# A ceiling on the planner's work per step: attention followed by a learned density, on one core

## The chip, the cores and the metric

The kernel runs on one core of a Trainium2 chip. The metric is device time in microseconds (us), the median of several executions. Beside the timed runs there is one profiled execution; all views below are of that one.

## What is computed

The input `x` has 8 images of 192 channels and 64 x 64 points, in float32. Two layers follow each other, each a group norm, a function and a residual:

```python
b, c, h, w = x.shape
q = prelu(conv1x1(x, w1, b1), a1)      # 24 channels
k = prelu(conv1x1(x, w2, b2), a2)      # 24 channels
v = prelu(conv1x1(x, wa, ba), aa)      # 192 channels
score = softmax(einsum('bnc,bcm->bnm', q, k), axis=2)   # 4096 x 4096
out = einsum('bnm,bmc->bnc', score, v)
...
# layer 1, for each channel, at xr - 0.5 and at xr + 0.5
for i in range(4):                      # widths 1, 3, 3, 3, 1
    logits = einsum('cij,cjn->cin', softplus(ms[i]), logits) + bs[i]
    if i < 3:
        logits = logits + tanh(fs[i]) * tanh(logits)
likelihood = maximum(abs(sigmoid(sign * upper) - sigmoid(sign * lower)), 1e-6)
...
x = x + attention(group_norm(x))
x = x + density(group_norm(x))
```

The attention is matmul work (TensorE), with an exponential for each score (ScalarE) and a row maximum (VectorE). The density is pointwise: chains of activations (ScalarE) and of multiply-adds (VectorE).

## The kernel before, in words

An image's attention is 8 blocks of 512 queries, and each block takes 16 steps of 256 keys: 128 steps an image, 1024 in all. One step `t` of the main loop emits, in this order: the score matmuls of step t + 1 into the one score buffer (`scores`, L780); the matmuls and the reduce of the maxima for a step 22 ahead (`max_step`, L708 and L716; one buffer too); the exponential of step t + 1 on ScalarE (L784), whose result `e` the values are multiplied with; the value matmuls of step t (`attend`, L795); and then everything else, in `work_off`.

Each engine works through its own queue in the order in which instructions were emitted. So what `work_off` puts on ScalarE in step t stands ahead of the exponential of the step after, and what it puts on VectorE stands ahead of the next reduce.

`work_off` sets out three kinds of work. *Due work* was entered with `at(t, fn, cost, act, pe)` for a given step, with planned prices for VectorE, ScalarE and TensorE: norms (L442 to L506), the evacuation of a finished block (L819), the residual (L837), the end of a density tile (tanhs and sign at L1202 and L1204, sizes L1249, stores L1254). `run_due` emits all that is due. A *job* needs a free PSUM bank and starts where one is found (`start_job`); the keys (L620), values (L669), output transposes (L828), turned maxima (L745) and folded weights (L547) of the next or current image are jobs, and their parts become due work of this step and the next ones. *Density work* fills up: `density_step` adds a rate to each engine's credit, and `Unit.step` emits operations while the credit is positive. Due work is taken from the same credit, and TensorE time beyond a plain step is added to it.

A `Unit` is one of 12 parts of an image's density (2 column halves, 3 channel groups, 2 sides), 128 x 1024 elements. It holds a list for ScalarE (17 activations: L1015 and L1024 from the input, L1030 tanh, L1040 scaled, L1072) and one for VectorE (22 multiply-adds, all at L1047). Up to three units are open at a time. An operation is emitted when what it reads was emitted in an earlier step, and when one of 17 buffers is free for it. The density of image b runs beside the attention of image b + 1. That of the last image has no attention beside it: its first mixes are matmuls (L988), and it makes the tail.

VectorE's rate is what is left of the image's density divided by the steps left, at most `MOST` = 3.3 a step; ScalarE's is 2.9. A credit can grow to the rate plus 1.3. The prices are 1.22 for a multiply-add, 1.23 for an activation, 1.05 for a tanh of a later layer. A step's own exponential and reduce are outside these sums.

Of the kernel before, what the change touches and what calls it, by code (L numbers as in the profile page):

```python
# [17 lines left out]
def kernel(  # L18
# [58 lines left out]
    last = B * IMG  # L77
# [40 lines left out]
    for i in range(3):  # L118
        t = xin.tile([128, 3, P], F32, tag=f"xi{i}", name=f"xi{i}")
# [211 lines left out]
        due.setdefault(max(t, now[0]), []).append((fn, cost, act, pe))  # L331

    credit = {"DVE": 0.0, "ACT": 0.0, "PE": 0.0}
    units = deque()
    jobs = []
    stream = [False]
# [40 lines left out]
    def start_job(t):  # L377
        p = t % STEPS
        for n, (rank, make, hold, banks, cols) in enumerate(jobs):
            if stream[0] and (p < 3 or p + max(hold, 1) >= STEPS):  # L380
                continue
            rooms = [(pm, g) for pm, g in homes if sum(k <= t for k in g) >= banks]
            if not rooms:
                if rank < 2:
                    return
                continue
            k = [i for i in (1, 0) if ready[i] <= t and scratch[i][0].shape[1] >= cols]
            if cols and not k:
                continue
            del jobs[n]  # L390
            pm, guest = min(rooms, key=lambda r: max(r[1]))
            at_ = [i for i in range(2) if guest[i] <= t]
            for i in at_[:banks]:
                guest[i] = t + hold + 1
            if cols:
                ready[k[0]] = t + 2
            spot[0] = next(n for n, k in enumerate(turns + others) if k is pm), at_[0]
            parts = make(pm if banks == 2 else pm[:, at_[0], :], scratch[k[0]] if cols else None)
            for i, fn, cost, act, pe in parts:
                at(t + i, fn, cost, act, pe)  # L400
            return
# [5 lines left out]
    def run_due(t):  # L407
        todo = due.get(t, [])
        i = 0
        while i < len(todo):  # L410
            fn, cost, act, pe = todo[i]
            fn()
            credit["DVE"] += pe - cost
            credit["ACT"] += pe - act
            i += 1
        due.pop(t, None)

    def work_off(t, rate):
        now[0] = t
        run_due(t)  # L420
        start_job(t)
        run_due(t)
        held = set()
        for kind, fn in list(loads):
            if free[kind] > 0 and kind not in held:
                loads.remove((kind, fn))
                fn()
            else:
                held.add(kind)
        density_step(t, rate)  # L430
        pool_step()
# [173 lines left out]
    for i in range(2):  # L605
        t = dram.tile([NC, 64, F], F32, tag=f"qd{i}", name=f"qd{i}")
# [259 lines left out]
    COST = {"DVE": 1.22, "ACT": 1.23, "TANH": 1.05, "PE": 6.95}  # L866
# [41 lines left out]
    class Unit:  # L908
# [192 lines left out]
        def step(self, eng, t, older):  # L1101
            todo = self.todo[eng]
            while todo and credit[eng] > 0:
                name, after, fn, makes, frees = todo[0]
                if any(self.at.get(a, t) >= t for a in after if eng != "DVE" or a[0] in "ltu"):
                    return
                if eng == "PE" and not banks:
                    return
                if makes and len(bufs) <= sum(u.need() for u in older) + len(endings):
                    return  # L1110
                todo.popleft()
                if makes:
                    self.take(name, makes)
                fn(name)
                self.at[name] = t
                for k in frees:
                    self.give(k)
                credit[eng] -= COST["TANH" if name[0] == "t" and name[1] else eng]

    def density_step(t, rate):  # L1120
        if units and t < last:

            left = sum(len(u.todo["DVE"]) for u in units if u.key[0] == units[0].key[0])
            rate = left * COST["DVE"] / max(1, (units[0].key[0] + 2) * IMG + 15 - t) + OTHER
            rate = min(rate, MOST)
        act = ACT_RATE if t < last else rate

        for eng, most in (("DVE", rate), ("ACT", act)):
            more = (rate if eng == "DVE" else 0.0) if t >= last else 1.3
            credit[eng] = min(credit[eng] + most, most + more)  # L1130
        credit["PE"] = min(credit["PE"] + rate, rate)
        for eng in ("ACT", "PE", "DVE"):
            order = list(range(min(3 if t < last else 4, len(units))))
            if len(units) == 2 and t < last:

                order.sort(key=lambda n: -len(units[n].todo["DVE"]))
            for n in order:
                units[n].step(eng, t, list(units)[:n])
        for u in [u for u in units if not u.busy()]:
            units.remove(u)  # L1140
# [17 lines left out]
    def pool_step():  # L1158


        if pieces:
            if len(recent) == 2:
                inst = nc.gpsimd.memset(pause, 0.0)  # L1163
                tc.add_manual_dep(
                    inst.ins, recent[0].ins.name,
                    mybir.DependencyInfo(
                        mybir.DependencyClass.Sync, mybir.DependencyReason.DATA
                    ),
                    reason="beside the reduce",
                )  # L1170
            pieces.popleft()()
# [184 lines left out]
    def go_on():  # L1356
        work_off(now[0], 0.0)
        now[0] += 1
# [40 lines left out]
    for t in range(last):  # L1399
        b = t // IMG  # L1400
        if t % IMG == 0:
            within(b, t)
            if b + 1 < B:
                prepare(b + 1, t)
            else:

                diagonals(0, t + 93)
                diagonals(1, t + 104)
                diagonals(2, last - 11)
        now[0] = t  # L1410
        if t % STEPS == 0:
            homes[:] = [(turns[(t // STEPS + 1) % 2], [0, 0])]
        if 3 < t < IMG:
            next(rest, None)
        assert t != IMG or next(rest, 0) == 0
        run = scores(t + 1) if t + 1 < last else None
        max_step(t + LEAD)
        if run:
            run()
        attend(t)  # L1420
        work_off(t, RATE - 1.215)
    t = last
    homes[:] = [(turns[1], [0, 0])]
    while due or units or jobs or loads:

        work_off(t, RATE if (B - 1, 1) in norms else 1.3)
        t += 1
# [38 lines left out]
```

## Time and profile before

| what | us |
|---|---|
| median of 3 runs (4797.65 to 4801.9) | 4800.04 |
| profiled execution, its time | 4801.53 |
| profiled execution, its span | 4799.7 |
| TensorE matmuls busy | 4653.4 |
| VectorE busy | 4179.0 |
| ScalarE busy | 3196.8 |
| end of the last exponential | 4440.9 |

The chain of waits, followed back from the last instruction, spends 86% of the span on TensorE, 7% on VectorE and 5% on ScalarE. The forty slices of the page show 9 tenths for VectorE from the seventh slice on, where the density of the first image begins, and 6 or 7 tenths for ScalarE. TensorE's granted clock is full nearly throughout.

| mean duration of one, ns | |
|---|---|
| exponential, L784 | 1021 |
| activation of the density, L1015, L1024, L1040 | 1236 to 1237 |
| later tanh, L1030 | 1054 |
| multiply-add, L1047 | 1292 to 1314 |
| reduce of the maxima, L716 | 1220 |

In the groups of instructions and in the timelines, a line gives the engine, the line of the kernel, the operation, and out<-in by the kernel's names; in brackets stands the idle time before it and what ended it. ACT is ScalarE, DVE VectorE, PE TensorE, POOL GpSimd. Neighbours on one engine overlap by a tenth of a microsecond or so, so the distance of two starts tells more of a queue than a duration does. Busy TensorE is a modelled figure: a matmul can be shown as running while it waits.

### The profile page before, as it was taken

What the parts mean: (1) busy time and instruction counts of PE and PEld (TensorE: products, weight loads), DVE (VectorE), ACT (ScalarE), POOL (GpSimd) and SP (SyncE); (2) the same over time, 40 slices, a digit from 0 to 9 for tenths busy, and PEclk for the clock granted to TensorE, in tenths of its full rate; (3) what the DMA queues carried; (4) which work ended last, traced back from release to release, by engine and by line L of the source; (5) the groups of instructions that cost most, each with busy time, mean ns of one, the idle gap of its engine ahead of it and who ended that gap; (6) DMA issues with size and microseconds to landing.
All of it is one profiled execution on the core that took longest, in us unless ns stands there. A gap on an engine that the chain in (4) does not pass through costs nothing.

```text
span 4799.7 us, 69014 instructions
## 1 busy us (share of the span) xinstructions
PE 4653.4 (97%) x28432; PEld 3440.0 (72%) x28432; DVE 4179.0 (87%) x4289; ACT 3196.8 (67%) x3665; POOL 856.3 (18%) x842
## 2 busy tenths in 40 slices
PE   7999999999999999999999999999999999999686
PEld 5777777777777777777777777777777777777332
DVE  5433359999999999999999999999999999998788
ACT  2333246777677767776777767777777777777675
POOL 0000001222122211221211221122222132222000
PEclk9999999999999999999999999999999999999898
DMA  2101020111110111010110111101111101000000
GB/s 58 41 18 29 18 48 14 35 28 29 42 27 25 37 39 34 27 44 9 36 46 26 33 40 33 32 19 33 36 38 33 34 13 27 10 12 16 9 13 13
DMA packets 109328, 138.60 MB, mean 29 GB/s; under 512 B 17106, under 2 KB 82132, under 8 KB 109012
## 3 DMA queue, kind: packets, MB, share of 16 engines
q1 hardware_dynamic: 107776, 133.81, 11.4%
q8 instruction: 223, 3.65, 0.3%
q14 instruction: 93, 0.76, 0.1%
q10 hardware_dynamic: 1236, 0.37, 0.0%
HBM read 100.58 MB, written 29.36 MB: 27 GB/s over the span
## 4 chain that ended last, share of the span: by engine, by line
PE 86%; DVE 7%; ACT 5%; issue 1%; DMA 0%; POOL 0%; ACTq 0%; SPq 0%; DVEq 0%; POOLq 0%
PE b L795 53%; PE sc L780 20%; PE b L669 4%; DVE d L1047 4%; PE b L988 2%; PE b L620 2%; DVE rm L716 1%; ACT d L1015 1%; ACT e L784 1%; PE mx_tail L988 1%; PE sc_tail L988 1%; PE b L828 1%; PE mx L708 1%; ACT d L1040 1%; PE b L745 0%
## 5 line engine op out<-in xcount | busy, mean ns | idle before, releaser
L795 PEld LDWEIGHTS b<-v,e 128*128 128x128 f32 x16384 | 2651.8, 190 | 776.9 <-issue 771.6
L795 PE MATMUL b<-v,e 128*128 128x193 f32 x16384 | 2955.7, 334 | 0.0
L784 ACT ACTIVATE e<-sc 128x1024 f32<-128x1024 f32 x1024 | 1045.9, 1021 | 1353.4 <-PE mx L708 1330.8
L716 DVE TENSOR_REDUCE rm<-mx 128x1 f32<-128x1024 f32 x1002 | 1222.3, 1220 | 481.4 <-PE mx L708 472.7
L780 PE MATMUL sc<-q,k 25*128 25x512 f32 x4096 | 1155.1, 640 | 24.2 <-ACT e L784 22.9
L708 PE MATMUL mx<-k,q 24*128 24x512 f32 x4008 | 1130.4, 640 | 0.6 <-DVE rm L716 0.6
L1047 DVE SCALAR_TENSOR_TENSOR d<-d,lc,d 128x1024 f32<-128x1024 f32 x756 | 986.1, 1314 | 12.2
L1047 DVE SCALAR_TENSOR_TENSOR d<-d,wsp,d 128x1024 f32<-128x1024 f32 x684 | 883.3, 1292 | 53.1 <-ACT d L1040 44.7
L1047 DVE SCALAR_TENSOR_TENSOR d<-d,tf,d 128x1024 f32<-128x1024 f32 x540 | 687.5, 1292 | 0.4 <-ACT d L1030 0.4
L1163 POOL MEMSET pause<- 128x1 f32 x408 | 40.0, 98 | 3613.2 <-DVE d L1047 3613.2
L1030 ACT ACTIVATE d<-d 128x1024 f32<-128x1024 f32 x540 | 568.2, 1054 | 42.6 <-DVE d L1047 40.8
L780 PEld LDWEIGHTS sc<-q,k 25*128 25x128 f32 x4096 | 306.2, 183 | 252.4 <-issue 175.8
L1040 ACT ACTIVATE d<-d,cb,wsp 128x1024 f32<-128x1024 f32 x348 | 429.9, 1236 | 4.3 <-DVE d L1047 3.3
L1015 ACT ACTIVATE d<-xc,bn,wn 128x1024 f32<-128x1024 f32 x288 | 354.0, 1236 | 7.7 <-issue 5.9
L1078 POOL TENSOR_TENSOR d<-d,d 128x512 f32<-128x512 f32 x168 | 331.8, 1975 | 47.7 <-ACT d L1072 46.6
L1024 ACT ACTIVATE d<-xc,bn,wn 128x1024 f32<-128x1024 f32 x252 | 311.8, 1237 | 0.0
L708 PEld LDWEIGHTS mx<-k,q 24*128 24x128 f32 x4008 | 299.8, 183 | 7.3 <-DVE rm L716 6.7
L1198 POOL TENSOR_TENSOR d<-d,d 128x512 f32<-128x512 f32 x80 | 173.0, 2163 | 0.0
L1210 POOL TENSOR_TENSOR d<-d,d 128x512 f32<-128x512 f32 x80 | 163.2, 2040 | 0.5 <-issue 0.5
L1218 POOL TENSOR_TENSOR d<-d,d 128x512 f32<-128x512 f32 x80 | 157.6, 1970 | 2.5 <-POOL pause L1163 0.9
L669 PE MATMUL b<-wv,xi 64*128 64x192 f32 x1344 | 139.5, 340 | 0.0
L669 PEld LDWEIGHTS b<-wv,xi 64*128 64x128 f32 x1344 | 106.5, 186 | 25.4 <-issue 21.5
(155 smaller groups left out, 2303.9 us busy)
## 6 DMA issues: line engine op xcount, KB each, us to landing
xi<-in_x_dram SPq DMA_DIRECT2D x280, 192.0 KB, 3.5
xc<-in_x_dram SPq DMA_DIRECT2D x64, 384.0 KB, 7.1
out_dram<-xc SPq DMA_DIRECT2D x94, 256.0 KB, 3.1
q<-qd SPq DMA_DIRECT2D x128, 128.0 KB, 2.7
k<-kq SPq DMA_DIRECT2D x64, 64.0 KB, 1.9
qd<-kq SPq DMA_DIRECT2D x64, 64.0 KB, 2.0
d<-in_x_dram SPq DMA_DIRECT2D x16, 192.0 KB, 4.1
out_dram<-xc SPq DMA_DIRECT2D x4, 128.0 KB
```

What stands on the lines that cost most here:

```text
L669: nc.tensor.matmul(pv[:, s, 0:C], lhsT=t[p, g, k * 128 : k * 128 + 128] if g < 3 else one_row[p], rhs=wf["v", b][p, g, :] if g < 3 else wf ...
L708: nc.tensor.matmul(sc[:, s, :], lhsT=tile_of(qt[b, n // 2], n, j)[r], rhs=kt[b][r, u : u + F], start=True, stop=True,)
L716: nc.vector.tensor_reduce(out=rowmax[b, n][:, j, k : k + 1], in_=sc, axis=AX.XY, op=ALU.max)
L780: nc.tensor.matmul(sc[:, s, :], lhsT=kt[b][r, k : k + 128], rhs=qt[b, n // 2][r, :, u : u + 256], start=True, stop=True,)
L784: return lambda: nc.scalar.activation(e, sc, AF.Exp)
L795: nc.tensor.matmul(a[:, j, 0 : C + 1], lhsT=e[:, s, j * 128 : j * 128 + 128], rhs=v[:, s, p % 4, :], start=p == 0 and s == 0 and j % 2 == ...
L1015: nc.scalar.activation(self.buf[k], self.src(), AF.Tanh, bias=bn[:, s, g, 0, i : i + 1], scale=wn[:, g, 0, i : i + 1],)
L1024: nc.scalar.activation(self.buf[k], self.src(), AF.Identity, bias=bn[:, s, g, 1, i : i + 1], scale=wn[:, g, 1, i : i + 1],)
L1030: nc.scalar.activation(self.buf[k], self.buf["l", k[1], k[2]], AF.Tanh)
L1040: nc.scalar.activation(self.buf[k], self.buf["l", n - 1, 0], AF.Identity, bias=offset, scale=wsp[:, g, w : w + 1],)
L1047: nc.vector.scalar_tensor_tensor(dst, src, factor, dst, ALU.mult, ALU.add)
L1078: return nc.gpsimd.tensor_tensor(z[:, n], z[:, n], dst[:, n], ALU.add)
```

## The change

Each step now keeps an account, `spent`, of what it has emitted for VectorE and ScalarE. It is set to zero at the start of `work_off`; due work adds its price less the TensorE time that it brings; a density operation adds its own price. Before a unit emits an operation, the sum with that operation is held against `FULL`, 4.0 for VectorE and 3.7 for ScalarE, and if it would be over, the unit stops for this engine and this step. What is left of the credit is carried on within the old limit of the rate plus 1.3. The ceiling is in force up to the last step of the attention, not in the tail, and due work is never held.

```diff
@@ -331,6 +331,9 @@
     credit = {"DVE": 0.0, "ACT": 0.0, "PE": 0.0}
+
+    spent = {}
+    FULL = {"DVE": 4.0, "ACT": 3.7}
     units = deque()
@@ -412,11 +415,14 @@
             fn()
             credit["DVE"] += pe - cost
             credit["ACT"] += pe - act
+            spent["DVE"] += cost - pe
+            spent["ACT"] += act - pe
             i += 1
         due.pop(t, None)
 
     def work_off(t, rate):
         now[0] = t
+        spent.update(DVE=0.0, ACT=0.0)
         run_due(t)
@@ -1108,6 +1114,9 @@
                 if makes and len(bufs) <= sum(u.need() for u in older) + len(endings):
                     return
+                cost = COST["TANH" if name[0] == "t" and name[1] else eng]
+                if t < last and spent[eng] + cost > FULL[eng]:
+                    return
                 todo.popleft()
@@ -1115,7 +1124,9 @@
                 for k in frees:
                     self.give(k)
-                credit[eng] -= COST["TANH" if name[0] == "t" and name[1] else eng]
+                credit[eng] -= cost
+                if eng in spent:
+                    spent[eng] += cost
```

## The prediction

> **What bounds the kernel now.** I read the page first: its busy row, then the chain of waits.
>
> ```profile
> PE 4653.4 (97%) x28432; PEld 3440.0 (72%) x28432; DVE 4179.0 (87%) x4289; ACT 3196.8 (67%) x3665; POOL 856.3 (18%) x842
> ```
>
> TensorE fills 97% and heads the chain of waits with 86%. A busy share doesn't tell how much of it is hidden waiting, so I looked for a rhythm. The longest pieces of the chain, in order of time, repeat one piece at each image's boundary:
>
> ```profile
> 1804.48 3.52 DVE d L1047 x3
> 2354.39 3.52 DVE d L1047 x3
> 2904.29 3.52 DVE d L1047 x3
> 3454.21 3.52 DVE d L1047 x3
> ```
>
> One image of 128 steps takes 549.9 us, four times alike. Now the matmuls alone. In TensorE's timeline a step is the distance between two first score matmuls (L780). A step with no other work takes 3.88 us. One with a values job (L669 x16) takes 5.38, keys (L620) 5.18, turned maxima (L745) 4.32, output transposes (L828) 4.54, a norm's matmul (L456, L471) 4.00, the folded weights (L547, L552) 6.28. An image holds 16, 8, 8, 8, 4 and 1 of these: 128 x 3.88 + 16 x 1.50 + 8 x 1.30 + 8 x 0.44 + 8 x 0.66 + 4 x 0.12 + 2.40 = 496.6 + 46.1 = 542.7 us. So 7.2 us of every image are stalls: that is all that a smoother queue can win there. Step by step the excess over these durations adds to 7.0 in a steady image (steps 384 to 895 of the 1024, four images), 4.3 in steps 128 to 255, 8.2 in 256 to 383, 2.9 in 896 to 1023: 43 us in all, 0.9% of the span.
>
> TensorE's own waits show only half of that:
>
> ```profile
> PE sc L780 <- ACT e L784: 22.9, 31, 2.3
> ...
> PE mx L708 <- DVE rm L716: 0.6, 4, 0.2
> ```
>
> The rest lies in matmuls whose modelled ends cover the wait. Here is a wait that shows, first ScalarE's timeline, then TensorE's (start, us, what):
>
> ```profile
> 2050.24 1.02 ACT L784 ACTIVATE e<-sc 128x1024 f32<-128x1024 f32 x1 [0.78 <-PE mx L708]
> 2051.16 0.83 ACT L596 ACTIVATE pra<-b,b 128x256 f32<-128x256 f32 x2
> 2051.87 1.16 ACT L1072 ACTIVATE d<-d,wsp 128x1024 f32<-128x1024 f32 x1
> 2052.91 1.24 ACT L1015 ACTIVATE d<-xc,bn,wn 128x1024 f32<-128x1024 f32 x1
> 2054.04 1.24 ACT L1024 ACTIVATE d<-xc,bn,wn 128x1024 f32<-128x1024 f32 x1
> 2055.18 1.23 ACT L1015 ACTIVATE d<-xc,bn,wn 128x1024 f32<-128x1024 f32 x1
> 2056.31 1.01 ACT L784 ACTIVATE e<-sc 128x1024 f32<-128x1024 f32 x1
> ```
> ```profile
> 2057.38 0.70 PE L780 MATMUL sc<-q,k 25*128 25x512 f32 x2 [0.54 <-ACT e L784]
> ```
>
> The exponential `e` frees the one score buffer. Between two of them the planner queued a due prelu (booked 0.9) and four density activations (4 x 1.23): 5.82 booked, 6.07 us from one `e` to the next. The scores come at 2057.38 where 2052.88 + 3.88 = 2056.76 was possible: 0.6 lost.
>
> VectorE has its own such place, at the boundary:
>
> ```profile
> 2352.67 1.22 DVE L716 TENSOR_REDUCE rm<-mx 128x1 f32<-128x1024 f32 x1
> 2353.81 0.58 DVE L451 BATCH_NORM_AGGREGATE mv<-st 128x2 f32<-128x96 f32 x1
> 2354.30 1.22 DVE L1047 SCALAR_TENSOR_TENSOR d<-d,tf,d 128x1024 f32<-128x1024 f32 x1
> 2355.44 1.28 DVE L1047 SCALAR_TENSOR_TENSOR d<-d,wsp,d 128x1024 f32<-128x1024 f32 x1
> 2356.63 1.28 DVE L1047 SCALAR_TENSOR_TENSOR d<-d,tf,d 128x1024 f32<-128x1024 f32 x1
> 2357.83 1.22 DVE L716 TENSOR_REDUCE rm<-mx 128x1 f32<-128x1024 f32 x1
> ```
>
> The step books 3 x 1.22 + 0.4 = 4.06; the reduce that frees the max buffer ends at 2359.05, and TensorE's step is 5.15, 1.27 too long.
>
> **The change part by part.** No instruction is added or removed, no transfer is touched; the counters are Python at build time. What changes is the step in which a density operation is emitted. SyncE's and GpSimd's queues get the same entries, those behind a moved operation some steps later; nothing that TensorE needs is behind them (the fetches keep their steps), so I cost that at nothing. If a store's delay held an `xc` buffer for longer, it would cost at most a late fetch; the slack there is tens of steps.
>
> *ScalarE's ceiling, 3.7.* I counted what was emitted between two exponentials, at the planner's prices, less TensorE's due credit. In a steady image 14 of 128 steps exceed 3.7, by about 20 operations. Seven of the 14 are ahead of a stall. A step offers 3.88 us, and `e` ends 1.62 ahead of the next scores (2051.26 against 2052.88): a lag up to 1.62 costs nothing. Four density operations take 0.92 + 4 x 1.13 = 5.44, 1.56 over, just covered: those steps stall by 0. With due work of 0.85 (two evacuations, 0.61 real) it is 2.17 over: 0.55 is late, and the trace has 0.50. Under the ceiling three operations take 4.31, 0.43 over; a run of three such steps, about what the credit allows, lags by 1.3, under 1.62. So the isolated bursts (0.50 + 0.17 + 0.61 + 0.50 + 0.18 = 1.96 an image) should go.
>
> Three steps hold table loads for a norm's square root (booked 2.8) or two due tanhs and a sign (2.0). They let in two, two and one density operations today, and after it none, one, none. For the later pair (1.9 us) each stall has 1.13 of density work right ahead of the late `e`: I take 1.5 saved. The earlier (0.47) lies where VectorE is back to back for 30 us; I take nothing, since the reduce is late next.
>
> A rule of the Trainium skill speaks against this part: "ScalarE: Activation LUTs", section "What ACT_TABLE_LOAD costs", gives 1283 ns and then a drain of about 1380 for each switch. Two switches would be 5.3 us, nearly twice what is booked; a step would overflow with no density work in it, and the 1.5 would shrink to about 0. The trace has the first number and not the second: load at 2387.26 (1.28), root at 2388.56, load at 2389.91 (1.28), `e` at 2391.20, 0.02 us between. Root and both loads are 2.76. I go by the row.
>
> *VectorE's ceiling, 4.0.* One or two steps of a steady image exceed it, one of them the 1.27 above. Without the third operation the reduce ends 1.2 earlier; that operation goes to the next step, where about 0.5 of lateness comes back: 0.8 saved.
>
> *What waits instead.* A held ScalarE operation holds those behind it in its unit's list, and VectorE's operations that read it start a step later. No row shows that. Below: zero, since three units are open and VectorE takes another's work. Above: a lost slot costs nothing while VectorE has idle time, 549.9 - 531.5 = 18.4 us an image by the sums over the three stretches (14 slots of 1.29), and 1.29 after that. I take new stalls of 1.0 an image, between 0 and 5.
>
> Sum for a steady image: 1.96 + 1.5 + 0.8 - 1.0 = 3.2, times 4 = 13. Steps 256 to 383 have the same kinds in larger size (8.2): 3.5. Steps 128 to 255, where a first burst of four (4.92) precedes 3.8 of stall: 2. The last: 1. Together 19.5 us.
>
> *The tail.* From 4440.9, the last `e`, the ceiling is off. Some 34 density operations of image 6 are left over; their number follows from the rate, which aims at 15 steps past the end, so it stays within about 5. At 1.29 each that is 6 us either way, taken at zero.
>
> The profiled execution's span is 4799.7, its time 4801.5, 1.5 over the median. 4799.7 - 19.5 + 1.8 = 4782.0; less 1.5, 4780.5, say 4780.
>
> The skill's "Perfetto Trace Analysis", section "Identifying the Most-Contended Engine", would read this otherwise: matmul occupancy is no measure of headroom, the share of weight loads is. That is 72%, and 28% of the span would be room, over 1300 us. The rhythm bounds what this schedule of matmuls can give back at 43. I use 43 as the floor of the range: 4757, with 6 of the tail 4751.
>
> **The rivals.** *It only moves the stalls.* The held operations join steps that are near full, and at the boundary VectorE, not ScalarE, sets the time. For it: 2.7 of the 7.0 are at the boundary under back-to-back VectorE work. Against it: the isolated bursts have light neighbours (ScalarE is busy 404.5 of 549.9). Then 1.96 less new stalls of 1.0, six times: about 6 us, 4794.
>
> *VectorE starves and then binds.* Held activations feed VectorE's chains. If each of the 20 costs one slot, 20 - 14 = 6 slots of 1.29 exceed the idle time: 7.7 an image against the 4.2 won, 3.5 lost, times 6 = 21 us: 4821; with 18 slots 1.0 lost, times 6: 4806. It decides from about 17 lost slots an image on; I give it 4813. For it: VectorE is 97% busy inside an image. Against it: three units offer work, and the rate may rise to 3.3 where by my count 2.6 is booked on average.
>
> *The whole room is won:* 4757 to 4765, if the shifted order meets no new full step.
>
> *It hardly acts:* excluded, 14 steps an image exceed the ceiling.
>
> **How the numbers follow.** A measurement tells about 0.2% from no change, 9.6 us. Forecast (4765 to 4790) 0.46; most of the room 0.12; stalls only moved 0.20; starved 0.22. Faster 0.58, same 0.20, slower 0.22. The range runs from 4753 to 4815; the likeliest case alone is 4765 to 4790.
>
> **What would show it.** Period of a steady image about 546.7 instead of 549.9; no ScalarE stretch of four density operations between two `e` inside the stream; the sum of L780's waits on `e` under 12 us; plain steps still 3.88; VectorE's busy sum unchanged. Wrong, if the period is longer with reduces running late throughout, or if the time from the last `e` to the end (358.8 us) has grown.

## The result, and the profile after

The median fell from 4799.89 us (six runs, 4797.54 to 4801.9) to 4774.03 us (six runs, 4772.65 to 4778.6), ratio 0.9948 with a 95% interval from 0.9938 to 0.9957. The profiled execution took 4772.86, its span is 4771.1: 28.6 less than the span before. Six lines were inserted above the loops, so L780 is now L786, L784 is L790, L1047 is L1053, L1015 is L1021.

The page's busy row of after:

```profile
PE 4654.9 (98%) x28432; PEld 3442.5 (72%) x28432; DVE 4162.7 (87%) x4289; ACT 3198.0 (67%) x3665; POOL 865.9 (18%) x842
```

The counts of instructions on the five engines are the same to the last one: it is the same work in another order. The busy times are nearly so; VectorE's is 16.3 us lower, its multiply-adds taking 1284 to 1298 ns on average instead of 1292 to 1314. Why was not followed. TensorE's waits inside the stream of steps, which showed 22.9 us on the exponential before:

```profile
PE sc L786 <- ACT e L790: 3.8, 4, 2.2
```

Four waits are left of 31. None of the maxima's matmuls waits for the reduce any more, but their weight loads still do, for 8.2 us against 6.7 before. The sums over three images in the middle, from first scores to first scores (after the span of the stretch: busy us of PE, PEld, DVE, ACT, POOL, then the granted clock):

```profile
1724.31:2272.76 548.45, 548.40 (x3484) 416.94 (x3483) 528.71 (x536) 404.14 (x464) 125.99 (x121) 1.00 0.13 32
2272.76:2819.55 546.79, 546.74 (x3485) 415.29 (x3483) 528.67 (x536) 404.18 (x464) 126.02 (x121) 1.00 0.13 33
2819.55:3366.33 546.78, 546.72 (x3485) 415.27 (x3483) 528.56 (x536) 404.42 (x464) 125.48 (x121) 1.00 0.13 32
```

An image takes 546.8 where it took 549.9; the first of the three is 1.7 longer for a reason told at the end. By steps (duration of each less that of a step with the same jobs), a steady image's stalls fell from 7.0 to 3.9 where no such disturbance is in it.

How the 28.6 us are spread: the last exponential ends at 4421.5 instead of 4440.9, so 19.5 come from ahead of it and 9.1 from the tail (349.6 instead of 358.8). Of the 19.5, the steps 128 to 895 give 16.2 (2.1, 4.9, then 1.4, 3.1, 3.1 and 1.5 an image), steps 896 to 1023 give nothing (0.3 lost), and 3.6 were won ahead of step 128, where no density exists and the change can't act.

The step that held the burst of four (it starts with the prelu on `pra`, step 71 of an image), after the change:

```profile
2586.40 1.02 ACT L790 ACTIVATE e<-sc 128x1024 f32<-128x1024 f32 x1 [1.35 <-PE mx L714]
2587.32 0.83 ACT L602 ACTIVATE pra<-b,b 128x256 f32<-128x256 f32 x2
2588.03 1.06 ACT L1260 ACTIVATE d<-d 128x1024 f32<-128x1024 f32 x1
2588.98 1.06 ACT L1036 ACTIVATE d<-d 128x1024 f32<-128x1024 f32 x1
2590.28 1.02 ACT L790 ACTIVATE e<-sc 128x1024 f32<-128x1024 f32 x1 [0.24 <-PE mx L714]
```

One density operation (L1036) beside two pieces of due work, and at both ends ScalarE waits for TensorE (1.35, 0.24) instead of the other way round. At the boundary VectorE's third operation is gone from its old step and back one step on:

```profile
2345.53 1.25 DVE L1053 SCALAR_TENSOR_TENSOR d<-d,tf,d 128x1024 f32<-128x1024 f32 x1
2346.70 2.66 DVE L1053 SCALAR_TENSOR_TENSOR d<-d,lc,d 128x1024 f32<-128x1024 f32 x2
2349.28 1.22 DVE L722 TENSOR_REDUCE rm<-mx 128x1 f32<-128x1024 f32 x1
```

These three (and a due 0.2 ahead of them: 3.86, under the ceiling of 4.0) make a step that is 1.10 too long, where it was 1.27.

### The profile page after: what moved, and what is told of

Read it like the earlier page. It is cut to its first block, busy times and chain, and to the rows that moved or that the text cites. A ratio compares the mean times of both kernels' runs of the same rounds, so it can differ in the third digit from the quotient of the medians.

```text
span 4771.1 us, 69026 instructions
## 1 busy us (share of the span) xinstructions
PE 4654.9 (98%) x28432; PEld 3442.5 (72%) x28432; DVE 4162.7 (87%) x4289; ACT 3198.0 (67%) x3665; POOL 865.9 (18%) x842
## 4 chain that ended last, share of the span: by engine, by line
PE 95%; ACT 2%; DVE 2%; DMA 0%; issue 0%; POOL 0%; ACTq 0%; SPq 0%; DVEq 0%; POOLq 0%
PE b L801 60%; PE sc L786 22%; PE b L675 4%; PE b L994 2%; PE b L626 2%; PE mx L714 1%; PE sc_tail L994 1%; PE mx_tail L994 1%; DVE d L1053 1%; PE b L834 1%; PE b L751 1%; ACT d L1046 0%; ACT d L1021 0%; ACT e L790 0%; ACT d L1002 0%
## 5 line engine op out<-in xcount | busy, mean ns | idle before, releaser
L790 ACT ACTIVATE e<-sc 128x1024 f32<-128x1024 f32 x1024 | 1045.4, 1021 | 1320.1 <-PE mx L714 1282.6
L786 PE MATMUL sc<-q,k 25*128 25x512 f32 x4096 | 1154.2, 640 | 4.1 <-ACT e L790 3.8
L1053 DVE SCALAR_TENSOR_TENSOR d<-d,lc,d 128x1024 f32<-128x1024 f32 x756 | 974.0, 1298 | 16.7 <-ACT d L1030 4.8
L1053 DVE SCALAR_TENSOR_TENSOR d<-d,wsp,d 128x1024 f32<-128x1024 f32 x684 | 876.2, 1284 | 50.6 <-ACT d L1046 42.5
L1053 DVE SCALAR_TENSOR_TENSOR d<-d,tf,d 128x1024 f32<-128x1024 f32 x540 | 685.7, 1287 | 0.4 <-ACT d L1036 0.4
L1036 ACT ACTIVATE d<-d 128x1024 f32<-128x1024 f32 x540 | 566.8, 1052 | 34.4 <-DVE d L1053 34.1
L786 PEld LDWEIGHTS sc<-q,k 25*128 25x128 f32 x4096 | 306.2, 183 | 229.6 <-issue 188.9
L1021 ACT ACTIVATE d<-xc,bn,wn 128x1024 f32<-128x1024 f32 x288 | 353.4, 1234 | 0.8 <-issue 0.8
L1084 POOL TENSOR_TENSOR d<-d,d 128x512 f32<-128x512 f32 x168 | 335.8, 1999 | 36.9 <-ACT d L1078 35.7
L1209 POOL TENSOR_TENSOR d<-d,d 128x512 f32<-128x512 f32 x80 | 170.2, 2127 | 0.0
L1221 POOL TENSOR_TENSOR d<-d,d 128x512 f32<-128x512 f32 x80 | 170.1, 2126 | 0.5 <-issue 0.5
L1229 POOL TENSOR_TENSOR d<-d,d 128x512 f32<-128x512 f32 x80 | 159.4, 1992 | 1.7
```

The source lines that it names most:

```text
L786: nc.tensor.matmul(sc[:, s, :], lhsT=kt[b][r, k : k + 128], rhs=qt[b, n // 2][r, :, u : u + 256], start=True, stop=True,)
L790: return lambda: nc.scalar.activation(e, sc, AF.Exp)
L1021: nc.scalar.activation(self.buf[k], self.src(), AF.Tanh, bias=bn[:, s, g, 0, i : i + 1], scale=wn[:, g, 0, i : i + 1],)
L1036: nc.scalar.activation(self.buf[k], self.buf["l", k[1], k[2]], AF.Tanh)
L1053: nc.vector.scalar_tensor_tensor(dst, src, factor, dst, ALU.mult, ALU.add)
L1084: return nc.gpsimd.tensor_tensor(z[:, n], z[:, n], dst[:, n], ALU.add)
```

## Experiments

All were timed beside the kernel before, whose medians there were 4799.7 to 4801.2. "Period" is steps 512 to 640 of the profiled execution, first scores to first scores; "tail" is from the end of the last exponential to the end of the span; "half-clock windows" are stretches of 3.41 us at half the granted clock between 100 us and the last exponential. Each makes its step about 1.7 us longer, and the periods of e1 and e8 hold one.

| run | ceilings VectorE / ScalarE | median, us | ratio to before (95%) | period | tail | half-clock windows |
|---|---|---|---|---|---|---|
| before | none | 4799.89 | | 549.9 | 358.8 | 3 |
| after | 4.0 / 3.7 | 4774.03 | 0.9948 (0.9938 to 0.9957) | 546.8 | 349.6 | 2 |
| e1 | none / 3.7 | 4790.53 | 0.9981 (0.9973 to 0.9988) | 550.5 | 359.5 | 1 |
| e2 | 4.0 / none | 4805.46 | 1.0013 (1.0006 to 1.0019) | 550.9 | 358.8 | 5 |
| e3 | density alone, 4.0 / 3.7 | 4791.51 | 0.9983 (0.9976 to 0.9991) | 549.9 | 352.9 | 2 |
| e4 | 4.0 / 3.7 to step 896 | 4783.18 | 0.9968 (0.9956 to 0.998) | 546.7 | 360.0 | 2 |
| e5 | 4.0 / 3.7 from step 896 | 4790.59 | 0.9981 (0.9972 to 0.999) | 549.9 | 347.2 | 3 |
| e6 | 4.0 / 3.0 | 4877.68 | 1.016 (1.0146 to 1.0174) | 562.7 | 361.0 | 1 |
| e7 | 3.7 / 3.7 | 4766.40 | 0.9929 (0.9916 to 0.9941) | 546.2 | 348.8 | 0 |
| e8 | 4.0 / 4.95 | 4792.12 | 0.9983 (0.9974 to 0.9991) | 549.9 | 358.3 | 4 |
| e9 | 3.7 / 3.6 | 4775.42 | 0.9948 (0.9936 to 0.9961) | 546.1 | 352.4 | 1 |
| e10 | 3.7 / 4.3 | 4778.59 | 0.9953 (0.994 to 0.9965) | 546.8 | 352.5 | 4 |
| e11 | 3.4 / 3.7 | 4809.70 | 1.0021 (1.0012 to 1.003) | 543.7 | 401.0 | 5 |
| e12 | 3.4, from step 768 3.7 / 3.7 | 4780.55 | 0.9956 (0.9942 to 0.997) | 543.7 | 352.4 | 7 |

**One ceiling at a time.** The first two runs each keep one of the two.

```diff
-    FULL = {"DVE": 4.0, "ACT": 3.7}
+    FULL = {"DVE": 99.0, "ACT": 3.7}
```

> Only ScalarE's ceiling (VectorE's set to 99). My theory: ScalarE's bursts ahead of the exponential are most of it; VectorE's ceiling is worth about 0.8 us an image at the boundary. A steady image's period 547.6 (after: 546.8), stream 14 us shorter than before; tail (last exponential to end) unknown between 349 and 359, so 4776 to 4787. Rival (VectorE sets the boundary, and the two ceilings work only together): period above 548.5, time above 4790.

Measured 4790.5, period 550.5: just inside the rival's range. ScalarE's ceiling alone won 2.2 and 4.5 in the first two images with density, then nothing in two of four steady images, and 1.1 in a third if its half-clock window is left out. In those three, the due tanhs of an ended density tile (2.0) and the due square root (2.8) came to fall into one step, 4.8 together: the two steps after it are 1.20 and 0.42 too long. The ceiling holds density work and never due work, so it can't do anything there. In the fourth the two stayed apart, and that image is as short as with both ceilings:

```profile
2824.70:3371.42 546.72, 546.57 (x3484) 414.84 (x3482) 528.91 (x536) 404.16 (x464) 126.31 (x122) 1.00 0.13 33
```

So the theory that the parts add up falls. That ScalarE's bursts are most of it does not: whether its ceiling wins hangs on which due work the new order brings together.

```diff
-    FULL = {"DVE": 4.0, "ACT": 3.7}
+    FULL = {"DVE": 4.0, "ACT": 99.0}
```

> Only VectorE's ceiling (ScalarE's set to 99). My theory: the isolated bursts of four activations stay, the table-load steps too; period 549.1 against 549.9 before, 4790 to 4798 with the tail. Rival (VectorE is the bound): period near 547, time under 4782.

Measured 4805.5: VectorE's ceiling alone makes it slower, which neither theory expected. 19 steps of an image are over ScalarE's 3.7 instead of 14, and the pair of table-load steps stalls for 3.6 instead of 1.9. Of the 6.6 us by which its profile is longer, 3.3 are two more half-clock windows. The two gains alone (9 less and 6 more) are far from the 26 of both.

**Due work in the account or not.**

```diff
-            spent["DVE"] += cost - pe
-            spent["ACT"] += act - pe
```

> The ceilings hold density work alone, due work is not counted. My theory: steps of four activations are cut (2.0 us an image), the steps with table loads and two densities are not (1.4 an image comes back), so period 548.2 and 4780 to 4788. Rival (due work need not be counted): period 546.8 and 4774 as after.

Measured 4791.5, period 549.9: worse than expected. In a steady image nothing is won, 15 of 128 steps are over 3.7 with due work counted, and both the boundary's 1.27 and a table-load pair of 2.4 are there. So what works is the sum of due and density work, as the change's words say.

**Where the tail's 9 us come from.** The two runs split the steps at 896, where the last image's attention begins.

```diff
-                if t < last and spent[eng] + cost > FULL[eng]:
+                if t < last - IMG and spent[eng] + cost > FULL[eng]:
```

> Ceilings in force up to step 896 only, not beside the last image's attention. Theory: the stream up to there is as after, and the tail's 9 us came from the order in which the last image's steps leave buffers and open units; the time from the last exponential to the end goes back to about 358, total about 4783. Rival (the tail's gain is fixed by what the earlier images leave over): tail 350, total 4774.

```diff
-                if t < last and spent[eng] + cost > FULL[eng]:
+                if last - IMG <= t < last and spent[eng] + cost > FULL[eng]:
```

> Ceilings in force only from step 896 on, beside the last image's attention. Theory: the tail's 9 us hang on the order of the last image's steps, so the stream is as before (period 549.9) and the time from the last exponential to the end is 350: about 4791. Rival (it takes the state that the earlier images leave): tail 359 and about 4800.

Both came as the first theory had it: 4783.2 and 4790.6, tails of 360.0 and 347.2. The tail is set in the main by the order of the last image's 128 steps; what the earlier images leave is worth 1 to 2 us (358.8 against 360.0, 349.6 against 347.2). TensorE's waits show it. In the kernel before, and in the first of the two, one product of the tail waits long for its input activation:

```profile
PE mx_tail L988 <- ACT d L1015: 21.0, 4, 14.2
```
```profile
PE mx_tail L994 <- ACT d L1021: 22.4, 4, 15.6
```

After, and in the second, that wait is short:

```profile
PE mx_tail L994 <- ACT d L1021: 5.9, 4, 2.1
```
```profile
PE mx_tail L994 <- ACT d L1021: 6.5, 4, 1.8
```

Part of it came back elsewhere: the products into `b` wait for the same activations for 19.5 us after, with one wait of 9.4, against 13.2 before. The 9 us are what is left of such shifts.

From the point where the products run on without a gap, the two tails are alike (274.2 us before, 273.6 after). Both ceilings are needed for it: with one, the tail is 359.5 or 358.8. Which buffer or unit of those 128 steps makes that activation late wasn't traced.

**ScalarE's ceiling, lower and higher.**

```diff
-    FULL = {"DVE": 4.0, "ACT": 3.7}
+    FULL = {"DVE": 4.0, "ACT": 3.0}
```

> ScalarE's ceiling lowered to 3.0: two activations a step without due work, one with up to 1.7, none with more. By the prediction's rival this is where VectorE starves: supply is about the 204 activations that an image needs. Then waits on the exponential nearly vanish, but VectorE's rate rises to its limit, leftovers reach the tail, and the time is 4795 to 4830. The other theory (the lower the smoother): period under 546, time under 4770.

Measured 4877.7, 78 us slower: the starved case, and far beyond the price put on it. TensorE waits for the exponential for 6.9 us in all; the waits of its weight loads show what came in its place (of e6, then of after):

```profile
PEld mx L714 <- DVE rm L722: 56.8, 107, 1.3
```
```profile
PEld mx L714 <- DVE rm L722: 8.2, 17, 0.8
```

VectorE's density work has become uneven: of an image's 128 steps 12 hold none and 45 hold three or more, against 5 and 36 after. A step of three makes the reduce late although VectorE is idle in other steps, and only 530.2 of 562.7 us busy. Lost slots were not free.

```diff
-    FULL = {"DVE": 4.0, "ACT": 3.7}
+    FULL = {"DVE": 4.0, "ACT": 4.95}
```

> ScalarE's ceiling at 4.95: four activations (4.92) fit when nothing is due, and not with an evacuation or prelu; due work is counted. My theory of a slack of 1.62 us ahead of the next scores: bare steps of four cost nothing, so only the table-load pair gets worse (4.28 is let in): period 547.8 in a steady image, 4778 to 4786 with the tail. Rival (each operation ahead of the exponential costs): period above 549, time above 4790.

Measured 4792.1, period 549.9: slower than my theory gave and just inside its rival's range. The one bare burst of 4.92 in that image (step 604) indeed stalls nothing, and the bursts with an evacuation are gone; but the pair of table-load steps costs 2.44, more than without any ceiling (1.91). In the other steps the stalls are no worse. And 1.6 of the period of 549.9 is a half-clock window; the steady image without one takes 548.2, near the 547.8 of my theory. So the rival's number came about without its cause.

**VectorE's ceiling, lower.**

```diff
-    FULL = {"DVE": 4.0, "ACT": 3.7}
+    FULL = {"DVE": 3.7, "ACT": 3.7}
```

> VectorE's ceiling at 3.7 instead of 4.0, so a step of three multiply-adds and a due 0.2 (3.86), which precedes the 1.10 stall at each boundary, is cut. If that third operation is the cause: period 545.7, about 4768. If VectorE's work at the boundary is simply too much for its steps, the stall only moves: period 546.5 to 547.5, 4772 to 4778. The tail may differ by up to 9 either way.

Measured 4766.4, the fastest of all, and 7.6 under after; in its profile the period is 546.2 in all four steady images. The step of 3.86 is gone with its 1.10; but 0.55 came back a step later, and 0.58 at an earlier step of the boundary, which went from 0.23 to 0.81. Together that is 1.13: at the boundary the stall moved and nothing was won. The 0.6 that an image gains lies with the table loads, where a stall of 0.54 is gone. About 3.3 us of the 7.6 are the two half-clock windows that this run doesn't have.

```diff
-    FULL = {"DVE": 4.0, "ACT": 3.7}
+    FULL = {"DVE": 3.7, "ACT": 3.6}
```

> VectorE 3.7 as in the run before it that was fastest, ScalarE 3.6: three plain activations (3.69) no longer fit in a step, two and a tanh (3.51) do. If runs of 3.69 cause what is left at the boundary (0.56 and 0.38 follow such steps): period 545.3, 4760 to 4766. If 3.6 is already towards the starved side (3.0 cost 100 us): VectorE gets steps of none and of three, period above 548, time above 4776.

Measured 4775.4, neither: the steady period is 546.1, as good as before it. The 0.38 and 0.56 at the boundary stayed though no step there holds three plain activations, so such runs of three aren't their cause. The 9 us were lost elsewhere: 3.6 in the tail, 3.4 in steps 0 to 255 (two half-clock windows), and 1.9 in one image in which the due 2.0 and 2.8 fell together again.

```diff
-    FULL = {"DVE": 4.0, "ACT": 3.7}
+    FULL = {"DVE": 3.7, "ACT": 4.3}
```

> VectorE 3.7, ScalarE 4.3: two tanhs and a due 2.0 (4.28) fit again, so the pair of table-load steps should get back its stall of 1.3 to 1.9 an image, and three activations fit with up to 0.6 due, which the slack covers: period 547.5 to 548, 4773 to 4781. If the clock and the tail decide and not these steps: 4766 within 4.

Measured 4778.6, period 546.8. The pair of table-load steps stalls for 1.26 where the run with 3.7 has 0.12, just under the low end of what was expected; other steps of the image give half of that back. The tail is 3.7 longer. That the time fell into the expected range is luck: of the 12.2 us over that run, 6.6 are its four half-clock windows.

```diff
-    FULL = {"DVE": 4.0, "ACT": 3.7}
+    FULL = {"DVE": 3.4, "ACT": 3.7}
```

> ScalarE 3.7, VectorE 3.4: three multiply-adds fit only in steps whose jobs give TensorE time back. An image needs 264 in 128 steps, two a step are 256, so it is near the least that suffices. Smoother reduces if it suffices: period 545 to 546, 4758 to 4768. If held operations pile up: leftovers in the tail, each 1.3 us, and a rate at its limit: above 4785.

Both halves of the expectation came true at once. One image reaches 543.7, 1 us over the bare matmuls' 542.7: nearly all its stalls are gone.

```profile
2271.29:2814.99 543.70, 543.70 (x3485) 413.64 (x3483) 522.97 (x533) 403.20 (x462) 123.50 (x118) 1.00 0.13 33
```

It held 261 multiply-adds in place of 264. The next image held all 264, and without its one half-clock window (1.6) it is as short (the span, then L1053 alone), so the smoothness isn't bought by doing less:

```profile
2814.99:3360.31 545.32, 332.01 (x264) 1.00 0.13 33
```

But 206 multiply-adds at L1053 come after the last exponential instead of 167, and the tail is 51 us longer. At 1.29 us each, the 39 more would make 50 us, as an estimate. Some 20 of them were left by the earlier images, the rest by the last one, whose steps held 244 in place of 260. In TensorE's waits it shows as one long wait of a product for its input activation:

```profile
PE b L994 <- ACT d L1021: 74.8, 6, 65.9
```

```diff
+        FULL["DVE"] = 3.4 if t < last - 2 * IMG else 3.7
```

> VectorE's ceiling 3.4 up to step 768, then 3.7; ScalarE 3.7. With 3.4 throughout, the steady images were the smoothest (period 543.5 to 546 against a floor of 542.7), and 39 operations more were left for the tail. If these leftovers pile up beside the last image alone: stream as smooth, tail back to about 350, 4757 to 4764. If they are carried on from image to image: tail above 365, time above 4775.

Measured 4780.6 with a tail of 352.4: neither was right. The leftovers are carried on, and were paid at once in the first image with the wider ceiling, not in the tail: steps 768 to 895 took 559.4.

```profile
3360.66:3920.01 559.35, 557.59 (x3484) 420.46 (x3483) 548.88 (x555) 417.81 (x476) 128.38 (x121) 0.99 0.13 32
```

VectorE is busy for 548.9 there and holds some twenty instructions more than an image's share: a debt that is paid back at once fills the steps. Two half-clock windows make 3.3 of the 559.4.

## Why the prediction was right, point by point

The range held, and most of the gain came the way that was forecast; how near the sum came is in part luck, as the last of these points shows.

*The bound and the room.* Right. The rhythm of bare matmuls (542.7 an image) held as the floor: the best image of any run took 543.5. The headroom that the weight loads' share of 72% would suggest isn't there; that share is still 72%.

*Table loads at 2.8 booked, not 5.3.* Right: with the ceiling the pair of steps dropped from 1.91 to 0.66 of stall. I had taken 1.5 and it was 1.25.

*Isolated bursts, 1.96 an image.* Right: all gone. What stands elsewhere in the image instead is 0.25 + 0.12 + 0.21 + 0.25 = 0.83, where I had taken new stalls of 1.0.

*The boundary, 0.8.* The size is right by luck. The whole boundary went from 3.12 to 2.37, but the step with the third operation, from which I had taken all of the 0.8, went from 1.27 to 1.10: the stall moved one step on nearly whole. Most of what was won is the stall of the earlier table-load step, 0.47, where I had taken nothing; it is still there with VectorE's ceiling alone.

*The count of bursts.* Eight, not seven, of the 14 steps over 3.7 are ahead of a stall: three with table loads or due tanhs and five isolated, as my own sums have them.

*A steady image, 3.2.* 3.1 in two of the four; the other two got a half-clock window each (1.7) and kept 1.5. In sum 9.2 instead of 13. The images ahead of them gave 7.0 instead of 5.5, the last 0.3 lost instead of 1 won. Of the stalls that I read there before (3.8 after the first burst of four, 8.2 in steps 256 to 383), 1.7 each are half-clock windows, which I had not told apart. They are gone after: 3.4 of the 7.0. Each stood behind a stall of over 2 us that the change cut, so their going may be its work.

*The tail, taken at zero and within 6.* Wrong, and this is the larger miss: 9.1. I bounded it by the number of leftovers, which did stay (166 multiply-adds after the last exponential, then 167). What changed was the order in which the last image's steps leave units and buffers, and with it one wait of 14 us, less the waits that grew in its place.

*Ahead of step 128.* 3.6 us of the difference are two half-clock windows (at 75 and 218 us of the span before) that the profile after doesn't have. That isn't the change's work as far as the views show.

So the forecast of 19.5 stands near the measured 25.9 with a miss up (tail and head, 12.7), a miss down (steady images, 3.8) and the rest as summed, in the profiled execution's 28.6. Put by cause, 15.8 of the 28.6 are stalls of the stream, against 19.5 forecast; 9.1 are the tail; and 3.7 are half-clock windows, five up to the last exponential before and three after. The prediction also summed the two ceilings as independent parts, and e1 and e2 show that they aren't: alone they give 9 less and 6 more.

*The rivals.* "It only moves the stalls" is true of VectorE's third operation at the boundary: moved, it took 1.10 of 1.27 along, and when the ceiling of 3.7 took that step away too, 1.13 came back for 1.10. Of ScalarE's isolated bursts it is true of less than half: 1.96 went and 0.83 came elsewhere. "VectorE starves" was put too far off: I let lost slots be free while VectorE had idle time, but with the ceiling at 3.0 it lost 78 us with 32 us idle an image, because idle time in one step doesn't help a full one.

## What to carry to other kernels

Where several queues must keep one engine fed, measure a period and subtract the bare work of the bound engine; that gives the room, which busy shares and the list of waits (23 of 43 us here) don't. A ceiling on work per step has to count all that stands in the queue, and it can be set too high, so that steps overflow, or too low, so that work is deferred, bunches up or lands in the tail. Whether a smaller limit of the credit would do as much as the ceiling wasn't tried. Such edits reorder everything behind them, so judge one by the stages it touches, and expect several us of luck where the schedule ends.

## What the runs showed of the hardware

A half-clock window costs more than many of the stalls here. The step that made the first of the three images above longer:

```profile
1845.71 4.56 PE L801 MATMUL b<-v,e 128*128 128x193 f32 x16
```

The same sixteen matmuls in the step after:

```profile
1851.27 2.88 PE L801 MATMUL b<-v,e 128*128 128x193 f32 x16
```

The sums over this stretch show the granted clock at 0.72 of full on average:

```profile
1845.00:1851.00 6.00, 6.00 (x32) 4.57 (x24) 4.76 (x9) 3.10 (x3) 0.00 (x0) 0.72 0.65 171
```

In the clock's records it is one stretch of 3.41 us at half speed, and a step with one is 1.64 to 1.68 too long. The Trainium skill ("TensorE: Matmul & The Clock Gate", section "What's actually happening") gives a free-running window of 3413 ns after which an idle array drops to half clock; the length agrees, but no idle stretch of that length shows ahead of one: the timeline lists no idle time of TensorE in the 10 us ahead of this one, and 2.09 us ahead of the one at 699.6 us in the kernel before. Where they come is plain from the fourteen profiles. Of eleven stalls of 2.0 us or more, ten have a window in the next step, and none of the stalls between 1.5 and 1.93 us has (the eight of e6 and one of e2). The step of the folded weights, with its two-column matmuls, has one behind it in 28 of 98 cases; the same schedule has it in two of four images. One more, in e12, stands behind a wait for a reduce in its own step, which is 3.8 too long. Between 0 and 7 of them fell into the runs' streams, so up to 12 us of a difference between two schedules can be theirs; e12 has seven, e7 none. What decides it behind the folded weights was not settled.
